# Two more products of q, k and v by quarters, shared PSUM banks, a later softmax quotient and another order in the last group

## The chip, the cores and the metric

The kernel runs on one core of a Trainium2 chip. Its time is the device time of one execution in microseconds (us); lower is better. The engines of the core are TensorE (PE in the profile, its weight loads PEld), VectorE (DVE), ScalarE (ACT), GpSimd (POOL) and SyncE (SP), which issues the DMAs. Each has its own queue of instructions and runs it in order; they meet by semaphores.

## The reference

There are 64 graphs of 256 nodes with 512 features, and one adjacency matrix for all. Layer 0 is a graph convolution, layer 1 an attention with 8 heads of 64 features, where the adjacency matrix makes an additive mask. Everything is fp32.

```
h = relu(layernorm(x))
x = x + (adj @ h) @ W0 + b0
h = relu(layernorm(x))
q, k, v = h @ Wq + bq, h @ Wk + bk, h @ Wv + bv
scores = q k^T / 8 + (1 - adj) * -1e9            # per head
x = x + softmax(scores) v @ Wo + bo
```

## The kernel before

**Groups.** Two graphs make a group (512 tokens), so there are 32 groups. Layer 0 runs over all of them first, then layer 1. In layer 1 the loop at L1132 repeats this order on PE, written out by hand: `attend(g, 0)`, `score(g, 1)`, q and k of group g + 1, `attend(g, 1)`, `score(g + 1, 0)`, v of g + 1, and the output projection o of g. The order in which the program names instructions is the order in each engine's queue (`manual_schedule`).

**Ticks.** Each of q, k, v, o is a Python generator with seven steps; after every step `tick()` advances a clock by one. `after(delay, fn)` puts a piece of work on a list, and the tick at which it is due names its instructions: behind that step's own instructions and ahead of the next step's, on whichever engines it uses. So a delay moves work in the queues of DVE, ACT and POOL against the steps of PE.

**Seven products.** A projection multiplies a 512 x 512 weight by 512 features of 512 tokens. Both are cut into halves, and seven half-size products (Strassen's scheme in Winograd's form) take the place of eight. With the weight's parts a11, a12, a22, s1 to s4 and the tokens' parts b11, b21, b22, t1 to t4 (block sums and differences), the products are P1 = a11 b11, P2 = a12 b21, P3 = s4 b22, P4 = a22 t4, P5 = s1 t1, P6 = s2 t2, P7 = s3 t3. `product` (L453) makes one of them by four matmuls of 256 columns. In groups 2 to 31 (`FIRST2`, L508) `project2` cuts P2, P3 and P4 once more by the same scheme: seven quarter-size products, each one matmul of 128 columns (L564), take the place of four matmuls of 256. This asks for more sums of weights (`block_sums`, once), of tokens (`Blocks.sums`, POOL, each group), and for more additions of results (`add`, L665, DVE; `first`, L907 and L924, ACT).

**Banks.** PSUM, where PE puts its results, has eight banks. `bank()` takes the one that has been free for longest, `give()` returns it. A bank asked for with `seed` has first a copy of SBUF data written to it by ACT (L255), and PE adds to that. `project2` holds at most six banks, one for each of its three inner products' common sums among them; `attend` holds two (`po`) for the unscaled result of the attention until `divide` has read them.

**The softmax.** `score` makes the scores (PE, L974), scales and masks them (DVE, L980, eight instructions), subtracts a bound (POOL, L986, four instructions of 128 x 1024), takes the exponential (ACT, L991, due at the ticks `exps`) and adds up pairs of keys (POOL, L998, due at `sum_delay` and the three ticks behind it). `attend` makes the denominators (PE, L1007) and the product with v (PE, L1014); ACT copies the denominators (L1023), DVE inverts them in four pieces (L1027), two at once and two in `divide`, where also the quotient is formed (L1045). `divide` is due one tick behind `attend`, that is behind the scores. `note` (ACT, L1039) sums up the reciprocals for a check of range.

**Buffers.** Input, residual and hidden tiles of 128 x 2048 come from a pool of four (`xpool`).

Of the kernel before, what the change touches and what calls it, by code (L numbers as in the profile page):

```python
# [13 lines left out]
P = 128  # L14
# [184 lines left out]
def kernel(  # L199
# [33 lines left out]
    main = ExitStack()  # L233
    const = main.enter_context(tc.tile_pool(name="const", bufs=1))
    dram = main.enter_context(tc.tile_pool(name="between", bufs=1, space=bass.MemoryType.DRAM))
    xpool = main.enter_context(tc.tile_pool(name="x", bufs=4))
    act = main.enter_context(tc.tile_pool(name="act", bufs=1))
    tmp = main.enter_context(tc.tile_pool(name="tmp", bufs=3))
    small = main.enter_context(tc.tile_pool(name="small", bufs=4))
# [8 lines left out]
    def bank(shape, name, seed=None):  # L248

        i = next(i for i in free_banks if seed is None or whole[i])  # L250
        free_banks.remove(i)
        t = psum.tile(shape, F32, tag=f"bank{i}", name=name)
        bank_of[id(t)] = (i, t)
        if seed is not None:
            nc.scalar.copy(t, seed[:, None, :].to_broadcast(shape))  # L255
        return t

    def give(t, all_written=True):
# [30 lines left out]
        return xt[32 * i:32 * i + 32, k * NT:(k + 1) * NT, :]  # L289

    def load(g):
        X[g] = xpool.tile([P, T, D], F32, tag="x", name=f"x_{g}")
        for k in range(GB):
            for i in range(NI):
                nc.sync.dma_start(blocks_of(X[g], i, k), by_block(x[g * GB + k], i))
# [212 lines left out]
    FIRST2 = 2  # L508
    W2, spare = {}, []

    def block_sums(n):

        todo = []
        for a in ONCE:
            w = W[n][a]
            def part(i, j):
                return w[:, j, i * P:(i + 1) * P]
            s1, s2, s4 = (spare.pop(0) for _ in range(3))
            W2[n, a] = dict(a11=part(0, 0), a12=part(0, 1), a22=part(1, 1), s1=s1, s2=s2, s3=part(1, 0), s4=s4)
            for o, p, q, op in ((s1, part(1, 0), part(1, 1), ALU.add), (s2, s1, part(0, 0), ALU.subtract),  # L520
                                (part(1, 0), part(0, 0), part(1, 0), ALU.subtract), (s4, part(0, 1), s2, ALU.subtract)):
                todo.append((nc.gpsimd.tensor_tensor, o, p, q, op))
        return todo

    class Blocks:

# [11 lines left out]
            eng.tensor_tensor(t[..., 2, :], self.operand("b22"), t[..., 0, :], op=op)  # L538
            eng.tensor_tensor(t[..., 3, :], self.operand("b21"), t[..., 2, :], op=op)

    def project2(n, halves, blocks, by_token, name, place, first, done=None, seeds=(), add_up=False):

        s = W[n]

        def part(t, i, k):

            m, h = (k, i) if by_token else (i, k)
            t = t if m is None else t[:, m:m + 1, :]  # L550
            return t.rearrange("p m (h j) -> p (m h) j", j=P) if h is None else t[:, :, h * P:(h + 1) * P]

        class Inner:

# [102 lines left out]
        for p, c in zip(inner, ((0, 0), (1, 0), (0, 1))):  # L657
            p.u3()
            p.add(p.sum, None, 1)
            give(p.shared, False)  # L660
            complete(*c)
        yield

    def add(o, ps, u):
# [187 lines left out]


    H1T, HH, HO = {}, {}, {}

    def load_hidden(g):
        H1T[g] = xpool.tile([P, GB, DC, N], F32, tag="x", name=f"h1T_{g}")
        for k in range(GB):
            nc.sync.dma_start(H1T[g][:, k].rearrange("p d n -> p (d n)").rearrange("p (i n) -> p i n", n=N // NI),
                              HT[g][:, :, :, k, :].rearrange("p d i n -> p (d i) n"))  # L860

    def load_residual(g):
        X[g] = xpool.tile([P, T, D], F32, tag="x", name=f"x1_{g}")
        nc.sync.dma_start(X[g], X1[g].rearrange("k (t p) d -> p (k t) d", p=P))

    def hidden_sums(g, *steps):
# [4 lines left out]

    H2, O2 = {}, {}

    def block_hidden(g, step):

        t = act.tile([P, GB, 4, P], F32, tag="t2", name=f"t2_{g}")
        t4 = act.tile([P, 4, P], F32, tag="t24", name=f"t24_{g}")
        x = H1T[g][:, :, 2:4, :].rearrange("p k c (n j) -> p k c n j", j=P)
        H2[g] = block_sums_of(x, t, HH[g], t4, nc.gpsimd, step)

    def block_outputs(g, eng, step):
        x = OT[g][:, 2:4, :].rearrange("p c (k n j) -> p k c n j", k=GB, j=P)
# [8 lines left out]
    def block_sums_of(x, t, halves, t4, eng, step):  # L891
# [3 lines left out]
        after(step + 1, last.sums, eng)  # L895
        return {"b21": Blocks(x[:, 0], t[:, 0]), "b22": Blocks(x[:, 1], t[:, 1]), "t4": last}

    def queries_keys(g):

        for n, store in (("q", Q), ("k", K)):  # L900
            store[g] = {}
            bias = L1[n][1]

            def first(o, ps, i, m=None):
                for c in range(2) if m is None else (m,):
                    to, src = (o[:, c, :], ps[:, c, :]) if m is None else (o, ps)
                    nc.scalar.activation(to, src, AF.Identity, bias=bias[:, 2 * i + c:2 * i + c + 1])  # L907

            def place(i, k):
                if (i, k) not in store[g]:  # L910
                    store[g][i, k] = act.tile([P, 2, N], F32, tag=f"{n}{i}{k}", name=f"{n}_{g}_{i}{k}")
                return store[g][i, k]

            if g < FIRST2:
                yield from project(W[n], HH[g], False, f"{n}_{g}", place, first)
            else:
                yield from project2(n, HH[g], H2[g], False, f"{n}_{g}", place, first)

    def values(g):
        v = act.tile([P, HQ, GB, NT, HF], F32, tag="yT0", name=f"v_{g}")  # L920
        V[g] = {(i, k): v[:, i, k] for i in range(HQ) for k in range(GB)}

        def first(o, ps, i, m=None):
            nc.scalar.copy(o, ps)  # L924

        def place(i, k):
            return V[g][i, k]

        if g < FIRST2:
            yield from project(W["v"], HH.pop(g), True, f"v_{g}", place, first)  # L930
        else:
            yield from project2("v", HH.pop(g), H2.pop(g), True, f"v_{g}", place, first)

    def quarter_of(batch, i):
        return batch.rearrange("(t p) d -> p t d", p=P)[:, :, i * HF:(i + 1) * HF]
# [64 lines left out]
    def attend(g, qd):  # L1000
# [25 lines left out]
        def invert(c):  # L1026
            nc.vector.reciprocal(rden[:, c * P:(c + 1) * P], den[:, c * P:(c + 1) * P])  # L1027

        early = 2 if g >= FIRST2 and (g, qd) != (NG - 1, 1) else 4
        for c in range(early):  # L1030
            invert(c)
        if qd == 0:

            last = g == NG - 1
            OT[g] = (xpool if last else act).tile([P, DC, GN], F32, tag="x" if last else "r", name=f"oT_{g}")
            HO[g] = Halves(f"o_{g}", [OT[g][:, :, k * N:(k + 1) * N] for k in range(GB)], 0 if last else 1)

        def note():
# [2 lines left out]
        def divide():  # L1041
            for c in range(early, 4):
                invert(c)
            for f in range(2):
                nc.vector.tensor_tensor(OT[g][:, 2 * qd + f, :], po[f], rden, op=ALU.mult)  # L1045
                give(po[f])
            after(2 if (g, qd) == (NG - 1, 1) else 3, note)
            wait = 0
            if qd == 0:
                HO[g].sums(nc.gpsimd, ("t1",))  # L1050
            elif g < NG - 2:
                HO[g].sums(nc.gpsimd, ("t3", "t2", "t4"))
            elif g == NG - 2:
                wait = 8
                after(7, HO[g].sums, nc.gpsimd, ("t3",))
                after(8, HO[g].sums, nc.vector, ("t2",))
                after(8, HO[g].sums, nc.gpsimd, ("t4",))
            else:
                HO[g].sums(nc.vector, ("t3", "t2"))
                HO[g].sums(nc.gpsimd, ("t4",))  # L1060
            if qd and g >= FIRST2:
                block_outputs(g, nc.gpsimd, wait + 1 if g >= NG - 2 else 2)

        after(1, divide)

    def run(gen, steps=99):

# [68 lines left out]
    for g in range(NG):  # L1136
        attend(g, 0)
        load_residual(g)
        if g + 2 < NG:
            load_hidden(g + 2)  # L1140
        score(g, 1, *((5,) if g < NG - 1 else (3, (3, 4, 5, 6))))
        tick()
        if g == 0:
            for n, tag in ((4 * DC, "w0_sb"), (4, "w0_s1"), (4, "w0_s2"), (4, "w0_s4"), (4, "adjT"), (4, "b0_r")):
                t = const.tile([P, n, P], F32, tag=tag, name=f"spare_{tag}")
                spare.extend(t[:, i, :] for i in range(n))
        for n, at in (("q", 7),) if g == 0 else (("k", 1), ("v", 5)) if g == 1 else (("o", 2),) if g == 2 else ():
            for i, work in enumerate(block_sums(n)):
                after(at + i // 3, *work)
        if g + 1 < NG:  # L1150
            run(queries_keys(g + 1))
        else:
            last = post(g - 1, seed_outputs(g - 1))
            run(last, 6)
        attend(g, 1)
        if g + 1 < NG:
            score(g + 1, 0, 5)
            tick()
            steps = values(g + 1)
            run(steps, 5)  # L1160
            seeds = seed_outputs(g) if g + 2 < NG else None
            run(steps)
            if g + 2 < NG:
                hidden_sums(g + 2, 2, 3, 4, 5)
                if g + 2 >= FIRST2:
                    block_hidden(g + 2, 6)
                run(post(g, seeds))
# [48 lines left out]
```

## Time and profile before

| | |
|---|---|
| time, median of 3 runs | 2661.51 us (2660.09 to 2661.95) |
| profiled execution: its own time | 2660.45 us |
| its span, first to last instruction | 2658.7 us |
| granted TensorE clock | 0.999 |
| layer 1, one group (group 13) | 63.0 us |
| of it q, k, v, o | 11.70 us each |
| of it a pair of scores / of attend | 3.65 us / 4.45 us, each twice |
| q, k, v of group 1 (no quarters) | 12.2 us each |
| from v of group 31 to the end | 55.8 us |

In a line of the profile, "128x512 f32<-128x512 f32 x4" is the shape of output and input (partitions x elements) and how many instructions there were; a group of lines in the timeline is merged, so "x2" behind a duration is two instructions in that time. What stands in square brackets is the time for which the engine had been idle before, and who ended that. One fp32 matmul of the program makes two records of PE. PE's ends are modelled, and the time by which one matmul follows another is the surer number.

### The profile page before, as it was taken

How to read it: one execution, taken by the hardware profiler on the slowest of the kernel's cores; microseconds unless marked ns; L12 is line 12 of the kernel's file. 1: busy time of each engine (PE TensorE's matmuls, PEld its weight loads, DVE VectorE, ACT ScalarE, POOL GpSimd, SP SyncE). 2: the span in 40 equal slices, each digit the busy share in tenths (PEclk: the TensorE clock that was granted, in tenths of full speed). 3: DMA queues.
4: the chain of work that ended last, by engine and by line, in shares of the span. 5: the costliest groups of instructions: out<-in, count | busy, mean ns of one | idle time of the engine just before them, and what ended most of it. 6: DMA issues, size and time to landing. Idle time of an engine off the chain costs nothing. (4 is left out here: it accounts for less than half of the span.)

```text
span 2658.7 us, 51781 instructions
## 1 busy us (share of the span) xinstructions
PE 2624.0 (99%) x20076; PEld 2282.2 (86%) x20076; DVE 1869.5 (70%) x3864; ACT 970.5 (37%) x1875; POOL 1981.1 (75%) x1838
## 2 busy tenths in 40 slices
PE   7999999999999999999999999999999999999997
PEld 6999899998888888888888888888888888888886
DVE  5878888885467676667677676667677676666677
ACT  3445454443333333333333333333333333333332
POOL 5888888775788777777777777777777777777775
PEclk9999999999999999999999999999999999999999
DMA  5777666665122111111111111111222111111110
GB/s 132 199 193 187 172 166 175 175 158 127 34 60 51 49 49 48 49 49 49 49 48 49 49 49 49 49 48 51 62 66 62 50 49 48 49 49 49 49 48 34
DMA packets 281066, 211.04 MB, mean 79 GB/s; under 512 B 145904, under 2 KB 212976, under 8 KB 280816
## 3 DMA queue, kind: packets, MB, share of 16 engines
q1 hardware_dynamic: 280352, 207.15, 29.9%
q8 instruction: 161, 2.64, 0.4%
q14 instruction: 89, 0.73, 0.1%
q10 hardware_dynamic: 464, 0.52, 0.1%
HBM read 106.96 MB, written 100.66 MB: 78 GB/s over the span
## 5 line engine op out<-in xcount | busy, mean ns | idle before, releaser
L986 POOL TENSOR_TENSOR a<-a,top 128x1024 f32<-128x1024 f32 x253 | 591.2, 2369 | 478.0 <-DVE a L980 478.0
L980 DVE SCALAR_TENSOR_TENSOR a<-sc,maskT 128x512 f32<-128x512 f32 x512 | 311.8, 680 | 122.8 <-PE sc L974 122.8
L998 POOL TENSOR_TENSOR as<-a 128x512 f32<-128x512 f32 x256 | 318.5, 1276 | 3.0 <-ACT a L991 3.0
L991 ACT ACTIVATE a<-a 128x1024 f32<-128x1024 f32 x256 | 270.9, 1058 | 4.3 <-DVE a L984 2.3
L1027 DVE RECIPROCAL rest<-rest 128x128 f32<-128x128 f32 x256 | 224.3, 919 | 36.1 <-ACT rest L1023 36.1
L974 PE MATMUL sc<-q,k 64*128 64x256 f32 x2048 | 239.0, 383 | 0.0
L1014 PE MATMUL pav<-a,v 128*32 128x256 f32 x4096 | 233.6, 379 | 0.0
L974 PEld LDWEIGHTS sc<-q,k 64*128 64x128 f32 x2048 | 194.7, 187 | 44.9 <-issue 26.3
L1014 PEld LDWEIGHTS pav<-a,v 128*32 128x32 f32 x4096 | 133.4, 110 | 87.9
L1023 ACT ACTIVATE rest<-pden 128x512 f32<-128x512 f32 x64 | 38.2, 597 | 417.7 <-PE pden L1007 417.7
L665 DVE TENSOR_TENSOR k<-k,k 128x128 f32<-128x128 f32 (+1 forms) x300 | 96.0, 352 | 126.3 <-PE k L564 123.9
L42 DVE BATCH_NORM_STATS2 st<-x 128x6 f32<-128x512 f32 x256 | 173.1, 676 | 9.4 <-DMA x<-in_x_dram 7.2
L693 ACT ACTIVATE h<-x,nb,rs 128x512 f32<-128x512 f32 x128 | 93.9, 803 | 69.3 <-POOL nb L54 69.2
L820 ACT ACTIVATE h<-x,nb,rs 128x512 f32<-128x512 f32 x128 | 97.2, 808 | 52.2 <-POOL nb L54 49.0
L665 DVE TENSOR_TENSOR x<-o,x 128x128 f32<-128x128 f32 (+1 forms) x360 | 110.9, 349 | 3.4 <-PE o_24b L564 0.3
L665 DVE TENSOR_TENSOR q<-q,q 128x128 f32<-128x128 f32 (+1 forms) x300 | 96.0, 352 | 14.0 <-PE q L564 11.7
L665 DVE TENSOR_TENSOR v<-v,v 128x128 f32<-128x128 f32 (+1 forms) x300 | 95.3, 351 | 14.4 <-PE v L564 11.3
L754 POOL TENSOR_TENSOR hs<-h 128x512 f32<-128x512 f32 x31 | 39.4, 1270 | 73.8 <-ACT h L693 63.7
L446 POOL TENSOR_TENSOR t_o<-oT,t_o 128x512 f32<-128x512 f32 x62 | 79.2, 1277 | 12.3 <-DVE t_o L446 10.0
L446 POOL TENSOR_TENSOR t_y<-yT 128x512 f32<-128x512 f32 (+1 forms) x65 | 81.8, 1258 | 5.9 <-ACT yT L804 5.9
L446 POOL TENSOR_TENSOR t_h<-h1T,t_h 128x512 f32<-128x512 f32 x64 | 82.0, 1282 | 5.0
L52 POOL TENSOR_TENSOR rs<-rs,mhalf 128x2 f32<-128x2 f32 (+1 forms) x97 | 79.5, 820 | 8.1
(4808 smaller groups left out, 6981.8 us busy)
## 6 DMA issues: line engine op xcount, KB each, us to landing
x<-in_x_dram SPq DMA_DIRECT2D x256, 128.0 KB, 3.1
residual<-x SPq DMA_DIRECT2D x256, 128.0 KB, 2.5
hidden<-r SPq DMA_DIRECT2D x128, 256.0 KB, 4.4
h1T<-hidden SPq DMA_DIRECT2D x64, 512.0 KB, 9.7
x<-residual SPq DMA_DIRECT2D x32, 1024.0 KB, 7.7
out_dram<-x SPq DMA_DIRECT2D x62, 512.0 KB, 4.3
w_sb<-in_L_gnn_weight_dram SPq DMA_DIRECT2D x1, 1024.0 KB, 9.8
wq_sb<-in_L_gnn_Wq_dram SPq DMA_DIRECT2D x1, 1024.0 KB, 8.2
```

What stands on the lines that cost most here:

```text
L42: nc.vector.bn_stats(st, src)
L446: eng.tensor_tensor(self.t[n][:, c, :], self.operand(p, c), self.operand(q, c), op=ALU.subtract)
L665: nc.vector.tensor_tensor(o, ps, u, op=ALU.add)
L693: nc.scalar.activation(H0[g][:, t, :], xt[:, t, :], AF.Relu, bias=nb[:, t % n:t % n + 1], scale=rs[:, t % n:t % n + 1])
L820: nc.scalar.activation(h1[:, k * NT + t, :], xt[:, k * NT + t, :], AF.Relu, bias=nb[:, t:t + 1], scale=rs[:, t:t + 1])
L974: nc.tensor.matmul(ps[j][:, kt * N:(kt + 1) * N], k[j * HD:(j + 1) * HD, c, kt * P:(kt + 1) * P], q[j * HD:(j + 1) * HD, c, :], start=(kt ...
L980: nc.vector.scalar_tensor_tensor(a[:, j * NT:(j + 1) * NT, :].rearrange("p k n -> p (k n)"), ps[j], SCALE, maskT_f, op0=ALU.mult, op1=ALU.add)
L986: nc.gpsimd.tensor_tensor(a, a, top_b, op=ALU.subtract)
L991: nc.scalar.activation(a, a, AF.Exp)
L998: nc.gpsimd.tensor_tensor(AS[c, b], a4[:, :, 0, :], a4[:, :, 1, :], op=ALU.add)
L1014: nc.tensor.matmul(po[f][h * 32:(h + 1) * 32, b * N:(b + 1) * N], v[:, k, h * HD + f * 32:h * HD + f * 32 + 32], A[h // 2, b][:, (h % 2) * ...
L1027: nc.vector.reciprocal(rden[:, c * P:(c + 1) * P], den[:, c * P:(c + 1) * P])
```

## The change

`project3` takes the place of `project2` for q, k and v of groups 2 to 31: P1 and P7 are made by quarters too, so five of seven products are, and only P5 and P6 stay half-size. The results of P1 and P7 are built in the outputs c00 and c11; the sums which P6 and P5 are added to are seeded by ACT from there. The running sums of P1, P7 and P3 (A1, A7, A3) share one bank, those of P2 and P4 (A2, A4) another. o keeps `project2`.

For this, two more block sums of tokens are made per group on POOL: `block_first` of b11, due twelve ticks behind the scores of qd 1, and in `block_hidden` those of t3, due two ticks ahead of those of b21 and b22. More weight sums are made (20 instructions in each of q, k and v instead of 12), those of k on DVE. Their room comes from the fourth x buffer, so that layer 1 turns three buffers (`next_x`). The bias of k and q is turned once into a difference.

`divide` is due four ticks behind `attend` where the next group uses `project3`, that is behind step three, all of it but the two early reciprocals. The exponentials are due at 5, 6, 6, 7 and the key sums from 7 on. In the last group the quotient of qd 0 is due a tick later, that of qd 1 at once; the sums of group 30's attention results are due at one tick, ahead of the last group's scores; five steps of o of group 30 stand ahead of the last `attend` where there were six.

```diff
-    xpool = main.enter_context(tc.tile_pool(name="x", bufs=4))
+    xpool = main.enter_context(tc.tile_pool(name="x", bufs=1))
...
+    BUILT = {"a11": "b11", "s3": "t3", **ONCE}
+    SECOND = {"q": BUILT, "k": BUILT, "v": BUILT, "o": ONCE}
...
+    def project3(n, halves, blocks, by_token, name, place, first):
...
+        def take(o, src, i, k, h):
+            first(part(o, i, k), src, h, i)
+
+        def own_added(o, t):
+
+            more(o, part(t, None, 0), None, 0)
+            more(o, part(t, 1, 1), 1, 0)
+
+        def own_taken(o, t, h):
+            first(part(o, None, 1), part(t, None, 1), h, None)
+            give(t)
+
+        c00, c01, c10, c11 = (place(i, k) for i in range(2) for k in range(2))
+        sa = bank([P, 4, P], f"{name}s")
+        a1, a7, a3 = (sa[:, i:i + 1, :] for i in range(3))
+        mm(a1, "a11", "a11", "b11", True)
+        mm(a7, "s3", "a11", "b11")
+        o1 = bank([P, 2, N], f"{name}o1")
+        own(o1, "a11")
+        o7 = bank([P, 2, N], f"{name}o7")
+        own(o7, "s3")
+        take(c00, a1, 0, 0, 0)
+        take(c11, a7, 0, 0, 1)
+        yield
+        mm(a1, "a11", "s2", "t2")
+        mm(part(o1, 1, 1), "a11", "s3", "t3")
+        mm(a7, "s3", "s2", "t2")
+        mm(part(o7, 1, 1), "s3", "s3", "t3")
+        mm(a3, "s4", "a11", "b11")
+        o3 = bank([P, 2, N], f"{name}o3")
+        own(o3, "s4")
+        take(c00, a1, 1, 0, 0)
+        take(c11, a7, 1, 0, 1)
+        take(c01, a3, 0, 0, None)
+        for o, t, h in ((c00, o1, 0), (c11, o7, 1)):
+            own_added(o, t)
+            own_taken(o, t, h)
+        yield
+        mm(a1, "a11", "s1", "t1")
+        mm(a7, "s3", "s1", "t1")
+        mm(a3, "s4", "s2", "t2")
+        mm(part(o3, 1, 1), "s4", "s3", "t3")
+        more(c00, a1, None, 1)
+        take(c01, a3, 1, 0, None)
+        pa = bank([P, 2, N], f"{name}a", seed=c00)
+        more(c11, a7, None, 1)
+        yield
+        o2 = bank([P, 2, N], f"{name}o2")
+        own(o2, "a12")
+        s24 = bank([P, 4, P], f"{name}s24")
+        a2, a4, c4 = (s24[:, i:i + 1, :] for i in range(3))
+        mm(a4, "a22", "a11", "b11", True)
+        mm(a2, "a12", "a11", "b11")
+        mm(a3, "s4", "s1", "t1")
+        take(c10, a4, 0, 0, None)
+        pc = bank([P, 2, N], f"{name}c", seed=c11)
+        more(c00, a2, 0, 0)
+        own_added(c01, o3)
+        yield
+        product(pa, s, "s2", halves, "t2", by_token, start=False, stop=False)
+        first(part(c10, 1, 0), part(pa, 1, 0), None, 1)
+        first(part(c10, None, 1), part(pa, None, 1), None, None)
+        more(c10, part(pa, 0, 0), 0, 0)
+        own_taken(c01, o3, None)
+        more(c01, a3, None, 1)
+        give(sa, False)
+        yield
+        own(pc, "a22", False)
+        mm(a2, "a12", "s2", "t2")
+        mm(part(o2, 1, 1), "a12", "s3", "t3")
+        mm(a4, "a22", "s2", "t2")
+        mm(c4, "a22", "s3", "t3")
+        more(c00, a2, 1, 0)
+        more(c10, a4, 1, 0)
+        more(c10, c4, 1, None)
+        more(c00, part(o2, 1, 1), 1, 0)
+        add(c00, o2, c00)
+        give(o2)
+        add(c10, pc, c10)
+        give(pc)
+        yield
+        product(pa, s, "s1", halves, "t1", by_token, start=False)
+        mm(a2, "a12", "s1", "t1")
+        mm(a4, "a22", "s1", "t1")
+        add(c11, pa, c11)
+        add(c01, pa, c01)
+        give(pa)
+        more(c00, a2, None, 1)
+        more(c10, a4, None, 1)
+        give(s24, False)
+        yield
...
+    def next_x():
+
+        turn[0] += 1
+        return f"x{(turn[0] - 1) % 3}"
...
+    def block_first(g, step):
+
+        x = H1T[g][:, 0, 0:2, :].rearrange("p c (n j) -> p c n j", j=P)
+        H2[g] = {"b11": Blocks(x, tmp.tile([P, 4, P], F32, tag="u", name=f"t11_{g}"))}
+        after(step, H2[g]["b11"].sums, nc.gpsimd)
...
+        H2[g]["t3"] = Blocks(HH[g].t["t3"].rearrange("p c (n j) -> p c n j", j=P),
+                             tmp.tile([P, 4, P], F32, tag="u", name=f"t33_{g}"))
+        after(step - 2, H2[g]["t3"].sums, nc.gpsimd)
...
+    def second(g):
+        return FIRST2 <= g < NG
...
+        delay = 4 if second(g + 1) else 2 if (g, qd) == (NG - 1, 0) else 1
...
             elif g == NG - 2:
-                wait = 8
-                after(7, HO[g].sums, nc.gpsimd, ("t3",))
-                after(8, HO[g].sums, nc.vector, ("t2",))
-                after(8, HO[g].sums, nc.gpsimd, ("t4",))
+                wait = 8 - delay
+                after(wait, HO[g].sums, nc.gpsimd, ("t3",))
+                after(wait, HO[g].sums, nc.vector, ("t2",))
+                after(wait, HO[g].sums, nc.gpsimd, ("t4",))
...
-        after(1, divide)
+        if (g, qd) == (NG - 1, 1):
+            divide()
+        else:
+            after(delay, divide)
...
-        score(g, 1, *((5,) if g < NG - 1 else (3, (3, 4, 5, 6))))
+        score(g, 1, *((7, (5, 6, 6, 7)) if second(g + 1) else (5,) if g < NG - 1 else (3, (3, 4, 5, 6))))
         tick()
+        if g + 2 < NG:
+            block_first(g + 2, 12)
...
-            run(last, 6)
+            run(last, 5)
         attend(g, 1)
         if g + 1 < NG:
-            score(g + 1, 0, 5)
+            score(g + 1, 0, *((5,) if not second(g + 1) else (7, (5, 6, 6, 7)) if g + 2 < NG else (5, (5, 6, 6, 7))))
```

In `project3`, `mm` is one quarter matmul, `own` makes three quarters of an inner product in a bank of its own, `more` is an addition on DVE (L665), `take` a copy or biased copy on ACT, and `part(t, i, k)` the quarter (i, k) of a tile (None for both).

## The prediction

> **What bounds the kernel now.** I read the page's busy table first, then PE's waits, then the timeline of one group of layer 1, because the change lies there.
>
> ```profile
> PE 2624.0 (99%) x20076; PEld 2282.2 (86%) x20076; DVE 1869.5 (70%) x3864; ACT 970.5 (37%) x1875; POOL 1981.1 (75%) x1838
> ...
> PE pa L331 <- DVE adj_p L326: 10.0, 1, 10.0
> PE o_30a L453 <- DVE x L665: 4.0, 1, 4.0
> PE pden L1007 <- POOL as L998: 2.9, 3, 1.3
> ```
>
> PE is never idle except at the start and in the last group: no wait on ACT or DVE stands in the 30 groups between. The chain of waits holds nothing but the last addition, so it gives no path; the order of PE's own work is the path. The stage table of group 13 (us, then PE, PEld, DVE, ACT, POOL busy) says the same: the whole group, then q, k, v, o.
>
> ```profile
> 1417.30:1480.30 63.00, 63.00 (x522) 54.29 (x520) 43.71 (x94) 21.29 (x45) 47.00 (x37) 1.00 0.21 51
> 1425.40:1437.10 11.70, 11.70 (x76) 10.79 (x75) 9.38 (x19) 7.18 (x16) 11.70 (x7) 1.00 0.60 117
> 1437.10:1448.80 11.70, 11.70 (x77) 10.82 (x75) 5.59 (x16) 4.69 (x11) 3.75 (x4) 1.00 0.00 0
> 1456.90:1468.60 11.70, 11.70 (x76) 10.80 (x75) 9.46 (x20) 7.22 (x15) 11.62 (x7) 1.00 0.01 1
> ```
>
> Each projection is 11.70 us of unbroken PE work. So fewer PE slots pay fully, and any new PE wait is paid fully. How such waits arise shows at the end of k of group 13:
>
> ```profile
> 1446.54 0.39 PE L564 MATMUL k<-t,wk_s 128*128 128x128 f32 x2
> 1446.97 0.62 ACT L907 ACTIVATE k<-k,bk_c 128x128 f32<-128x128 f32 x2 [3.31 <-PE k L564]
> 1447.44 0.39 PE L564 MATMUL k_13a<-h1T,spare_w_s 128*128 128x128 f32 x2
> 1447.88 0.39 PE L564 MATMUL k_13a<-t,wk_s 128*128 128x128 f32 x2
> 1448.31 0.37 ACT L907 ACTIVATE k<-k_13a,bk_c 128x128 f32<-128x128 f32 x1 [0.71 <-PE k_13a L564]
> 1448.71 0.62 DVE L665 TENSOR_TENSOR k<-k_13a,k 128x128 f32<-128x128 f32 x2 [0.20 <-ACT k L907]
> ```
>
> ACT at 1448.31 reads the quarter that the matmul of 1447.44 wrote, yet starts only 0.04 us after the last of three matmuls into that bank. DVE at 1448.71 reads other columns of the bank and still starts 0.03 us after ACT's read. At 1446.97 ACT reads the sum, but waits for the later s3 t3 into its shared bank. Order is kept per bank, reads against reads too.
>
> **What the Trainium skill says.** PSUM — Partial Sum Buffer, section "PSUM bank collisions raise a hardware error", tells authors to guard PSUM by bank, not by address, ScalarE reads against VectorE reads included; the lines above agree. The same page, "Engine vs sequencer instructions": ScalarE, VectorE and GpSimd queues are strict FIFO and matmuls start in program order; in the trace too nothing overtakes a waiting instruction. TensorE: Matmul & The Clock Gate, "Wait — 56ns, not 53.3ns?": a warm 128-column matmul takes 55.6 ns of which 2.5 is fixed. Here a quarter matmul's slot is 0.2225 us (four times that), a half product of four 256-column matmuls 1.725.
>
> **The change, part by part.** (1) *PE slots.* A half product by quarters is 7 x 0.2225 = 1.56 instead of 1.725: 0.167 less. Groups 0 and 1, which use no quarters, have 12.18 us per projection against 11.70 with three, so 0.163 each; I take that. Two more in q, k and v: 0.98 us per group, 29.4 us in 30 groups.
>
> (2) *The bank of A1, A7, A3.* I number the projection's matmuls from its start: 35 quarter slots and two half products, 35 x 0.2225 + 2 x 1.725 = 11.24 without a stall. Steps 1 and 2 have eight slots each; A3's first product is slot 12, at 12 x 0.2225 = 2.67, and to be seen at 2.67 + 0.39 + 0.04 = 3.10. The three ACT reads of A1, A7, A3 are issued behind it and so wait for it. In q and k two biased reads and a copy: the pair of 1446.97 took 0.62 with 0.36 for the last, so 0.26 each, and 0.26 for the copy, end 3.89; in v copies 0.17 apart (a pair takes 0.43), end 3.70. Step 3 begins with A1 in this bank, due at 3.56. A restart costs 0.15:
>
> ```profile
> 2624.70 0.73 POOL L539 TENSOR_TENSOR rest<-oT,rest 128x256 f32<-128x256 f32 x1
> 2625.48 0.49 PE L564 MATMUL o_30b<-wo_sb,rest 128*128 128x128 f32 x2 [0.21 <-POOL rest L539]
> ```
>
> Release at 2625.43, weights 0.05 later, and the first record 0.10 longer than 0.275. Stalls: 4.04 - 3.56 = 0.48 in q and k, 0.29 in v: **1.25 a group**. The 0.67 us of A3's other matmuls behind slot 12 is all the cover there is.
>
> (3) *Step 4.* In step 3 DVE adds A1 (0.42), ACT copies A3 (0.26), DVE adds A7 (0.42), by turns on one bank. A3 of step 3 is to be seen at 4.91 (q); then 5.36, 5.70, 6.16, so PE may write A3 at 6.31 against 6.04 due: 0.27 in q and k, 0.22 in v by the same count: **0.76**. Zero if ACT and DVE may read together.
>
> (4) *The quotient.* Behind step 3, DVE's queue gets two reciprocals and two products, with step 4's additions behind them:
>
> ```profile
> 1427.86 1.75 DVE L1027 RECIPROCAL rest<-rest 128x128 f32<-128x128 f32 x2
> 1429.64 1.29 DVE L1045 TENSOR_TENSOR oT<-pav,rest 128x512 f32<-128x512 f32 x2
> 1429.97 1.06 ACT L991 ACTIVATE a<-a 128x1024 f32<-128x1024 f32 x1
> ```
>
> From 6.07 on: 7.82, 9.14, then A2's first addition (0.28, 0.08 of it overlapped) until 9.34. PE's step 6 adds to A2 at 6.53 (step 4's end) + 1.725 + 0.67 = 8.92; released it starts at 9.49: 0.57 in q, the same in v, nothing in k (no quotient there): **1.14**.
>
> (5) *ACT in a bunch.* Exponentials now come behind steps 4, 5, 5, 6, three of them behind the copy of o3, which waits for DVE (10.0 in q). 10.4 plus three of about 1.0 plus the quotient's note (0.61 to the next start) is 13.8. k starts at 11.24 + 1.32 = 12.56, and its second A1 is due at 14.34; but ACT's two first reads of k end at 14.42, and PE restarts at 14.57: 0.23. In v the two seeds of o stand behind two of the exponentials: 12.57 against v's end at 12.32: 0.40. **0.63**, with 0 to 2 as bounds.
>
> (6) *The rest.* DVE gains per projection 2 additions of 128, 3 of 256 and 2 of 512, less one of 384 (0.28, 0.42, 0.69, 0.56): 2.6 us, 43.7 to about 51.5 of a longer group; cover enough but for (4). POOL gains two block sums of 0.73 + 0.46 + 0.46 = 1.65: the first falls into an idle stretch of 15 us in k; the second moves the end of POOL's backlog from q's start to about 1 us into q, whose first use is at 3.3. Cover gone, that is 1 us a group. Key sums stay ahead of the denominators by about 2 us. The three x buffers make the hidden load wait for the previous group's stores (4.3 us, then 9.7 to land) on SP's queue; first use is some 27 us after: nothing. Residual loads stand ahead of it in that queue. Weight sums: 24 more of about 0.46, once, off PE: nothing, up to 5 us. The bias subtraction: nothing. Banks: six and the two of the quotient, eight in all, no spare.
>
> (7) *Last group.* From 2602.9 to the end PE is busy 40.6 of 55.8 us. The DVE sum t2 moves ahead of the scores, the quotient behind step 1's addition (the 4.0 us wait), and g 30's block sums into idle POOL time, so the key sums end about 5 us earlier; one step more of o_30 covers the last quotient. DVE still does 3.0 of quotient and 2.1 of subtraction ahead of step 3's addition, a wait of some 2.7. I take -6, bounds -10 to 0.
>
> **Sum.** 1.25 + 0.76 + 1.14 + 0.63 - 0.98 = 2.80 us per group, 84 in 30. Against the profiled execution, 2660.45 us (span 2658.7): 2660.45 + 84 - 6 = 2738. The median 2661.51 is 1.06 above it, less than the spread of the runs.
>
> **Rivals.** *A, faster:* the reads hide in cover. PE has no wait in 30 groups before, and ACT is busy 37%, which speaks for it; the per-bank order above speaks against. It decides at one place: if the three reads are over by 3.41 (3.56 - 0.15), step 3 has no stall and all behind it moves forward. Then 2660.45 - 29.4 - 6 = 2625. *B, only (2) and a smaller (4):* ACT and DVE read side by side, so (3) goes, the quotient starts earlier (0.37 in q and v) and (5) fits: 1.25 + 0.74 - 0.98 = 1.0, 2685. The 0.20 us wait of DVE on ACT speaks against. *C, ACT becomes the bound at every border:* late exponentials make late key sums, and the denominators wait as in the last group (1.3 us at most there, twice a group): some 50 us more, 2788.
>
> **Numbers.** Forecast 0.48 (its own range 2705 to 2765), A 0.17, B 0.22, C 0.10, no change 0.03 (0.2%, about 5 us, is what a measurement of this kernel can tell from none). Range 2645 to 2770: it leaves out most of A and of C. Faster 0.17, same 0.03, slower 0.80.
>
> **What would show it.** PE waits on ACT before step 3 in q, k, v (0.3 to 0.5), on DVE before step 4's A3 and, in q and v alone, before step 6's A2 (0.6); a projection of 12.4 to 12.7 us. No such waits and 11.37 us means A; waits in step 3 alone mean B. The per-bank reading is what would make it wrong: if ACT starts before slot 12 is done, most of the sum falls.

## The result: slower by 3.3%

The changed kernel takes 2748.98 us (median of 4 runs, 2747.48 to 2749.42) beside 2661.73 us of the kernel before on the same chip (2660.09 to 2662.95): a ratio of 1.0327, interval 1.0309 to 1.0345. The profiled execution has a span of 2747.4 us at a granted clock of 0.997. The forecast was 2738.

First the page's busy table and PE's list of waits, of the changed kernel (total us, number of waits, longest):

```profile
PE 2675.0 (97%) x21156; PEld 2313.4 (84%) x21156; DVE 2091.8 (76%) x4426; ACT 1089.6 (40%) x2445; POOL 2082.5 (76%) x2022
...
PE pa L331 <- DVE adj_p L326: 9.6, 1, 9.6
PE q_2s L682 <- ACT q L1052: 2.6, 2, 2.0
...
PE pden L1156 <- POOL as L1147: 2.3, 3, 1.0
...
PE o_30a L453 <- DVE x L786: 2.1, 1, 2.1
...
PE v_4s L682 <- DVE v L786: 0.3, 1, 0.3
PE v_28s L682 <- DVE v L786: 0.3, 1, 0.3
PE q_5s L682 <- DVE q L786: 0.3, 1, 0.3
```

PE's share falls from 99 to 97%, and its busy time has even grown by 51 us, though its work shrank: with modelled ends part of a wait counts as busy (the last experiment below, with the same matmuls and hardly a wait, has 2596.4). The wait list looks harmless: its tile names hold the group's number, so one wait of 0.3 us that comes back in every group is spread over dozens of small rows. The stage table of one group shows it at once. These are group 13 whole, then its q, k, v, and the output o of group 12 (us, then PE, PEld, DVE, ACT, POOL busy, clock, DMA share, GB/s):

```profile
1453.08:1518.87 65.79, 64.58 (x558) 55.30 (x557) 50.65 (x113) 25.26 (x64) 50.24 (x43) 1.00 0.19 49
1461.19:1473.89 12.70, 12.17 (x89) 11.18 (x88) 10.68 (x26) 8.13 (x20) 12.54 (x9) 1.00 0.51 100
1473.89:1486.19 12.30, 12.07 (x89) 11.05 (x87) 8.32 (x23) 6.06 (x19) 5.63 (x7) 1.00 0.00 1
1494.30:1507.08 12.78, 12.33 (x89) 11.15 (x87) 10.95 (x26) 7.64 (x19) 11.81 (x7) 1.00 0.00 1
1507.08:1518.87 11.79, 11.79 (x75) 10.84 (x75) 8.57 (x22) 2.05 (x4) 11.48 (x13) 1.00 0.01 1
```

The group was 63.00 us and is 65.79, with 2.79 more: 1.00 in q, 0.61 in k, 1.08 in v, 0.10 in o. Attention and scores have not moved. The timeline of q of group 13 at the border of steps 2 and 3 shows the first of the new waits:

```profile
1463.97 0.39 PE L682 MATMUL q_13s<-h1T,wq_s 128*128 128x128 f32 x2
...
1464.39 0.63 ACT L1052 ACTIVATE q<-q_13s,bq_c 128x128 f32<-128x128 f32 x2 [1.83 <-PE q_13s L682]
...
1464.64 0.39 PE L682 MATMUL q_13o<-t,wq_s 128*128 128x128 f32 x2
...
1464.91 0.26 ACT L1049 COPY q<-q_13s 128x128 f32<-128x128 f32 x1
1465.22 0.30 PEld L682 LDWEIGHTS q_13s<-t,spare_w_sb 128*128 128x128 f32 x2 [0.39 <-ACT q L1049]
1465.23 0.38 PE L682 MATMUL q_13s<-t,spare_w_sb 128*128 128x128 f32 x1 [0.20 <-ACT q L1049]
```

The matmul of 1463.97 is A3's. ACT had been idle for 1.83 us, and the last matmul into A1, which it reads first, began at 1463.08; yet it starts at 1464.39, when A3's matmul is over. It doesn't wait for all that the program names ahead of it: o3's three matmuls stand ahead of the read too, and the last of them begins only at 1464.64. Its third read ends at 1465.17, and only then step 3 may write A1. The matmul of 1464.64 has two records 0.11 apart, so the next was due at 1464.86; it comes 0.36 later and its first record is 0.10 too long: 0.47 us lost.

The second new wait comes in step 4 of the same q, where A3 is written again:

```profile
1466.27 0.42 DVE L786 TENSOR_TENSOR q<-q_13s,q 128x256 f32<-128x256 f32 x1
1466.75 0.27 ACT L1049 COPY q<-q_13s 128x128 f32<-128x128 f32 x1
1467.05 0.42 DVE L786 TENSOR_TENSOR q<-q_13s,q 128x256 f32<-128x256 f32 x1 [0.35 <-ACT q L1049]
1467.53 0.49 PE L682 MATMUL q_13s<-t,spare_w_sb 128*128 128x128 f32 x2
```

These are DVE's read of A1, ACT's of A3, DVE's of A7 and the matmul into A3. A3's own reader ends at 1467.02, ahead of the 1467.34 at which the matmul was due. But DVE waits for that reader before it reads A7, until 1467.47, and PE starts 0.06 later; with its first record 0.10 too long, 0.29 us are lost.

The same q at step 6, where A2 is written again:

```profile
1469.18 1.29 DVE L1195 TENSOR_TENSOR oT<-pav,rest 128x512 f32<-128x512 f32 x2
...
1470.38 0.28 DVE L786 TENSOR_TENSOR q<-q_13s,q 128x128 f32<-128x128 f32 x1
1470.58 0.41 DVE L786 TENSOR_TENSOR q<-q_13o,q 128x256 f32<-128x256 f32 x1
1470.72 0.49 PE L682 MATMUL q_13s<-t,spare_w_sb 128*128 128x128 f32 x2 [0.31 <-DVE q L786]
```

DVE's first read of A2 (1470.38) stands behind the quotient and ends at 1470.66; 0.06 later PE starts. The three matmuls before began at 1469.58, so it was due at 1470.25; with a first record again 0.10 too long, 0.57 us are lost.

### The profile page after: what moved, and what is told of

It is laid out like the page before. It is cut to its first block, busy times and chain, and to the rows that moved or that the text cites. A ratio compares the mean times of both kernels' runs of the same rounds, so it can differ in the third digit from the quotient of the medians.

```text
span 2747.4 us, 54804 instructions
## 1 busy us (share of the span) xinstructions
PE 2675.0 (97%) x21156; PEld 2313.4 (84%) x21156; DVE 2091.8 (76%) x4426; ACT 1089.6 (40%) x2445; POOL 2082.5 (76%) x2022
## 5 line engine op out<-in xcount | busy, mean ns | idle before, releaser
L1140 ACT ACTIVATE a<-a 128x1024 f32<-128x1024 f32 x256 | 260.7, 1055 | 3.3 <-POOL a L1135 3.2
L446 POOL TENSOR_TENSOR t_o<-oT 128x512 f32<-128x512 f32 x63 | 81.0, 1286 | 29.5 <-DVE oT L1195 29.5
L947 DVE STREAM_TRANSPOSE r<-h 128x512 f32<-128x512 f32 x128 | 82.8, 684 | 2.1 <-ACT h L941 1.7
L1195 DVE TENSOR_TENSOR oT<-pav,rest 128x512 f32<-128x512 f32 x128 | 82.3, 685 | 2.1
```

Of the source, the lines that this page charges most:

```text
L446: eng.tensor_tensor(self.t[n][:, c, :], self.operand(p, c), self.operand(q, c), op=ALU.subtract)
L1140: nc.scalar.activation(a, a, AF.Exp)
```

## Experiments

The kernel before, timed again beside each of these runs, has medians between 2659 and 2661 us; ratios are given against them. "Group" is the mean period of groups 3 to 30 in the profile, from q to q: 63.02 us before, 65.81 after.

**A3 three slots later: is order kept by bank or by address?**

```diff
-        mm(a3, "s4", "a11", "b11")
         o3 = bank([P, 2, N], f"{name}o3")
         own(o3, "s4")
+        mm(a3, "s4", "a11", "b11")
```

> The changed kernel with step 2's A3 matmul behind the three of o3 instead of ahead of them: one line moved by three slots of 0.22 us, nothing else. Theory (order by bank): ACT may not read A1 and A7 before A3's matmul has written the bank, 0.67 us later than now, so step 3 waits 0.67 us longer in each of q, k and v: 2.0 us in each of 29 groups, about 2808 us, between 2795 and 2820. Rival (order by address): the reads of A1 and A7 start at once as they would with A3 in another bank, and step 3's wait stays or falls: 2749 or less.

2806.26 us (2804.62 to 2809.12), 1.0551, interval 1.0533 to 1.0568; group 67.82, or 2.01 more. The timeline of q of group 13 in this kernel:

```profile
1486.21 0.39 PE L682 MATMUL q_13s<-h1T,wq_s 128*128 128x128 f32 x2
1486.64 0.63 ACT L1052 ACTIVATE q<-q_13s,bq_c 128x128 f32<-128x128 f32 x2 [2.50 <-PE q_13s L682]
...
1487.15 0.27 ACT L1049 COPY q<-q_13s 128x128 f32<-128x128 f32 x1
...
1487.47 0.38 PE L682 MATMUL q_13s<-t,spare_w_sb 128*128 128x128 f32 x1 [0.87 <-ACT q L1049]
```

ACT's idle time grew by just the 0.67 us by which A3 was moved, and so did PE's wait. A read of A1 waits for a matmul that has nothing to do with A1 but the bank. Order by address is refuted. One PSUM tile of the program fills a bank here, so an order by tile would look the same. (The wait is one on a semaphore, and the program decides what it waits for; whether the chip itself would have needed it, this run doesn't tell.)

**A3 one step later in the same bank.** Its three matmuls go from steps 2, 3, 4 to 3, 5, 6, and two quarters of step 6 to step 4; A7's matmul of step 2 goes a slot earlier. Steps 2 to 4 in short:

```diff
-        mm(a3, "s4", "a11", "b11")
...
-        take(c01, a3, 0, 0, None)
...
-        mm(a3, "s4", "s2", "t2")
+        mm(a3, "s4", "a11", "b11")
...
-        take(c01, a3, 1, 0, None)
...
         more(c11, a7, None, 1)
+        take(c01, a3, 0, 0, None)
...
-        mm(a3, "s4", "s1", "t1")
+        mm(part(o2, 1, 1), "a12", "s3", "t3")
+        mm(c4, "a22", "s3", "t3")
...
-        own_added(c01, o3)
```

Step 5 gets A3's second matmul behind `product` and `own_added(c01, o3)`, step 6 its third.

> The changed kernel with A3's three matmuls one step later each, in the same bank, and the fourth quarters of A2 and A4 two steps earlier; the same matmuls, adds and copies. Theory (reads and matmuls of one bank are kept in order, so A3 between the reads of A1 and A7 makes step 3 and step 4 wait): the waits at step 3 (0.47, 0.47, 0.29 us) and step 4 (0.29, 0.29, 0.27) go, step 6's gets shorter by about 0.3 in q and v, while the late starts of k and o grow by about 1 us together because ACT has the two copies of o3 later; about 1.5 us less in each group, 2705 us, between 2690 and 2725. Rival (order by address, the waits come of DVE and ACT being late in general): no gain from moving A3, 2745 or more.

2695.77 us (2693.75 to 2698.77), 1.0139, interval 1.0122 to 1.0156; group 63.96, or 1.85 less. In q, k and v of group 13 the waits at steps 3 and 4 are gone; what is left is 0.34 at step 6 of q (0.57 in the changed kernel), 0.60 in k's first reads and 0.99 at the start of o. So the two bank waits go, and what ACT has to do late grows, as expected; the gain is 0.35 a group larger than expected.

**All reciprocals at the attention, so that the quotient is short.**

```diff
-        early = 2 if g >= FIRST2 and (g, qd) != (NG - 1, 1) else 4
+        early = 4
```

> The changed kernel with all four reciprocals of a quotient issued right behind the attention, so that behind step 3 only the two products of 0.65 us stand (about 1.3 us of DVE instead of about 3). Theory (the long quotient behind step three holds back the DVE reads of step 4, hence step 6's A2, and bunches the ACT reads ahead of k and o): the step-6 wait of about 0.57 us in q and v and the late starts of k (0.18) and o (0.39) go, 1.7 us in each of some 29 groups; about 2698 us, between 2685 and 2712. Rival (the stalls are only the bank order of A1, A7 and A3, and the quotient's length is idle filler): 2749 within 5 us. Rival (the reciprocals delay the reads of the scores, which stand behind them on DVE): 2755 or more.

2697.26 us (2696.80 to 2698.97), 1.0143, interval 1.0126 to 1.0159; group 64.09, or 1.72 less. The waits of steps 3 and 4 stand unchanged (0.47 and 0.28 in q). The timeline of q of group 13 at the quotient and step 6:

```profile
1447.31 1.28 DVE L1195 TENSOR_TENSOR oT<-pav,rest 128x512 f32<-128x512 f32 x2
...
1448.50 0.28 DVE L786 TENSOR_TENSOR q<-q_13s,q 128x128 f32<-128x128 f32 x1
...
1450.16 0.39 PE L682 MATMUL q_13s<-t,spare_w_sb 128*128 128x128 f32 x2
```

DVE reads A2 1.4 us ahead of PE's need, and step 6 has no wait. q is 0.58 shorter, k 0.19, v 0.85, o 0.10: the terms of the step-6 wait and of the late starts. The reciprocals cost nothing at their new place, where DVE waits for the scores.

**The quotient back behind the attention.**

```diff
-        delay = 4 if second(g + 1) else 2 if (g, qd) == (NG - 1, 0) else 1
+        delay = 1 if second(g + 1) else 2 if (g, qd) == (NG - 1, 0) else 1
```

> The changed kernel with the quotient one step behind the attention again (two reciprocals and two products ahead of step 2's reads) instead of behind step 3. Theory (DVE's reads of o1 and o7 in step 2 come 3 us late, and with them the reads of A1 and A7 that step 3 and step 4 wait for; in exchange the waits at step 6 and at the starts of k and o go): 2.7 us more in q and in v, about 2.4 us more in each of 29 groups on balance, 2819 us, between 2795 and 2840. Rival (the quotient behind step three is what makes the kernel slower): 2735 or less.

2803.61 us (2802.97 to 2805.13), 1.0535, interval 1.0517 to 1.0552; group 67.62, or 1.81 more where 2.4 was expected. In q of group 13 step 4 now waits 2.05 us for DVE in place of 0.29; step 6 and the starts of k and o wait no more. q grows by 1.18, v by 0.92. The 2.7 that was expected for q and v is too much: it is near the whole of the stalls (2.5 in q) and not their growth. With the quotient at its full length, the later place is the better of the two in this kernel.

**Both edits together**, and ACT's copy of o3 moved one step ahead of DVE's additions.

> Both edits, and the ACT copy of o3's right column moved one step ahead of its DVE adds. Theory: no wait is left inside q, k and v in a steady group, so that only the saving of 0.98 us in each group stands against the kernel before; 2749 less 3.8 times 29, about 2640 us, between 2630 and 2660, faster than the kernel before by 0.5 to 1.1%. Rival (DVE and ACT, which carry the adds and copies of two more quarter-size products, bound the projections themselves): the waits come back at other places, 2690 or more.

2648.16 us (2647.13 to 2650.16), 0.9957, interval 0.9940 to 0.9973: faster than the kernel before. The group is 62.40. In group 13 this leaves 0.31 in k (its first two reads stand behind the note on ACT's queue) and 0.09 in o of group 12 (PE waits for a sum of POOL). DVE and ACT have the same work as in the changed kernel, so their load was not the bound (DVE 50.1 us and ACT 25.3 in a group, against 50.7 and 25.3).

**The work ahead of group 2.** Its q took 17.2 us, 4.5 more than the later ones. The timeline of the changed kernel there, from two narrow windows; a merged row's end is its start and its us together:

```profile
733.39 4.79 POOL L1135 TENSOR_TENSOR a<-a,top 128x1024 f32<-128x1024 f32 x2
734.50 1.26 DVE L1065 TENSOR_TENSOR bq_c<-bq_c 128x2 f32<-128x2 f32 x1
735.69 2.63 DVE L276 TENSOR_TENSOR wk_sb<-wk_sb 128x128 f32<-128x128 f32 x2
735.80 0.37 ACT L1052 ACTIVATE q<-q_2s,bq_c 128x128 f32<-128x128 f32 x1 [2.55 <-DVE bq_c L1065]
...
735.89 4.79 DVE L276 TENSOR_TENSOR wk_sb<-wk_sb 128x128 f32<-128x128 f32 x2
738.14 2.40 POOL L1135 TENSOR_TENSOR a<-a,top 128x1024 f32<-128x1024 f32 x1
```

The subtraction of two columns takes 1.26 us and holds ACT, whose second read of q needs the new bias. Then two sums of k's weights end at 738.32 and 740.68, each some 0.15 us behind the end of a POOL instruction (738.18 and 740.54). Their ends follow POOL's and not their own size (0.28 us alone), so DVE doesn't slow down there; it stands still until POOL is done (the last section has this for more sizes). The Trainium skill says so: SBUF — State Buffer, section "Who interferes with whom", has a VectorE instruction with two SBUF inputs and a GpSimd one that reads SBUF exclude each other for the whole of an instruction. Behind these sums stand DVE's reads of q.

```diff
-                if g == FIRST2:
-
-                    nc.vector.tensor_tensor(bias[:, 2:4], bias[:, 2:4], bias[:, 0:2], op=ALU.subtract)
...
+            for n in "qk":
+                row = L1[n][1]
+                after(20, nc.vector.tensor_tensor, row[:, 2:4], row[:, 2:4], row[:, 0:2], ALU.subtract)
...
-        for n, i, at in ((("q", 0, 4), ("q", 1, 9), ("k", 0, 9)) if g == 0 else
-                         (("k", 1, 1), ("v", 0, 3), ("v", 1, 8)) if g == 1 else
+        for n, i, at in ((("q", 0, 4), ("q", 1, 9), ("k", 0, 9), ("k", 1, 20)) if g == 0 else
+                         (("v", 0, 3), ("v", 1, 8)) if g == 1 else
```

> The changed kernel with the two bias subtractions and the in-place sums of k's weights done by DVE while group 1's values run, instead of at the head of group 2. Theory (group 2's late start is these DVE instructions, two to five times longer beside POOL's mask subtraction, ahead of the reads of q's and k's first products): q of group 2 falls from 17.2 to about 12.8 us and k from 13.3 to 12.3, the kernel by 4 to 6 us to about 2744; the sums take what they may at their new place, where project needs DVE less. Rival (group 2 starts late because its own block sums or the weights' sums on POOL come late): q of group 2 stays above 16 us.

2742.90 us (2741.71 to 2746.45), 6.1 less than the changed kernel's 2748.98; 1.0312, interval 1.0295 to 1.0329. In the profile, from q of group 2 to q of group 3 it is 64.6 us and no longer 70.8; q of group 2 takes 12.1, k 12.1. At the new place DVE waits for POOL no less, as its instructions there tell (ns min/median/max):

```profile
L276 DVE TENSOR_TENSOR wk_sb<-wk_sb x4: 280/1055/1359, 707.8 to 711.2; 128x128 f32<-128x128 f32 x4
L276 DVE TENSOR_TENSOR bq_c<-bq_c x1: 1125/1125/1125, 706.7 to 706.7; 128x2 f32<-128x2 f32 x1
```

but POOL's instructions there are sums of 1.3 us and not subtractions of 2.4. The place isn't free either. DVE's additions for the output of group 0 stand behind these sums, and PE's list of waits has a new row:

```profile
PE o_0a L453 <- DVE x L786: 1.1, 1, 1.1
```

This output takes 13.5 us in place of 12.2, so of the 6.2 us won in group 2 some 4.9 remain; the 6.1 between the medians can't be told from that.

**The last group's order as it was.**

```diff
-        delay = 4 if second(g + 1) else 2 if (g, qd) == (NG - 1, 0) else 1
+        delay = 4 if second(g + 1) else 1
...
-            after(3, note)
+            after(2 if (g, qd) == (NG - 1, 1) else 3, note)
...
-        if (g, qd) == (NG - 1, 1):
-            divide()
-        else:
-            after(delay, divide)
+        after(delay, divide)
...
-            run(last, 5)
+            run(last, 6)
```

> The changed kernel with the last group's order as it was: six steps of group 30's output ahead of the last attention, its quotient one step later, the note as before. Theory (the other order saves less than the 6 us forecast, because the time that it takes out of group 30's output, 4.8 us, comes back in the last attention and in the last output): from the start of the last group's first attention to the end 49.1 us in place of 47.5, the kernel 1 to 2 us longer, 2750 or 2751, which the times alone can't tell from 2749. Rival (the forecast's 6 us): 53 us and 2755.

2747.10 us (2746.07 to 2747.49), 1.0322, interval 1.0305 to 1.0339, and in the profile from the last group's first attention to the last matmul (the tail) 45.0 us in place of 47.5. Both the theory (49.1) and its rival (53) had it longer. The other order costs 2.4 us in the profiles (the medians are 1.9 apart): with it the last attention comes earlier and PE waits there 1.1 us for key sums, a wait that the old order doesn't have. What the tail gained on the kernel before came from something else. One thing left of the change there is that group 30's sums t2, t4 and its block sums are due a step earlier, ahead of the last scores. That alone, in the kernel before:

```diff
-                after(8, HO[g].sums, nc.vector, ("t2",))
-                after(8, HO[g].sums, nc.gpsimd, ("t4",))
+                after(7, HO[g].sums, nc.vector, ("t2",))
+                after(7, HO[g].sums, nc.gpsimd, ("t4",))
...
-                block_outputs(g, nc.gpsimd, wait + 1 if g >= NG - 2 else 2)
+                block_outputs(g, nc.gpsimd, 7 if g == NG - 2 else wait + 1 if g == NG - 1 else 2)
```

> The kernel before with group 30's last sums of the attention output and their block sums one step earlier, as the change has them: ahead of the last group's second scores instead of behind them. Theory (this earlier start is what the tail gains, 4.1 us by the difference of the kernel before, 49.1, and e_last_order, 45.0): from the last group's first attention to the end 45 us, group 30's output from 16.1 to about 14 us, the kernel about 4 us shorter, 2656. Rival (the tail gains by the shape of the new projections or by the score's later exponents): the tail stays at 48 us or more.

2654.03 us (2653.45 to 2657.27), 0.9977, interval 0.9968 to 0.9986 (3.7 to 8.5 us less): in the profile the tail is 44.5 in place of 49.1, group 30's output 13.95 in place of 16.12. In its list of waits the 4.0 us of before have become

```profile
PE o_30a L453 <- DVE x L665: 2.2, 1, 2.2
```

**A kernel that beats both.** e_best has both edits of the projection, the earlier work for group 2, the first note of a group two steps later, and the last group's DVE subtraction of its first scores on POOL; the second run puts the last group's order back as well.

> e_a3_moved_recips and three more moves: the note of the first quotient of a group two steps later (out of the way of k's first two reads), the work before group 2 as in e_group2, and the last group's third mask subtraction on POOL as in the other groups. Theory: k's last wait (0.29 us in each of 29 groups, 8.4 us) goes, with about 4.5 us of group 2 and 1.4 us of the last group's values: 2648 less 14, about 2634 us, between 2628 and 2644; steady group 62.1 us. Rival (the note falls on another wait of k, and the sums collide with other work in group 1): 2645 or more.

2632.66 us (2631.50 to 2633.56), 0.9892, interval 0.9876 to 0.9909.

> e_best with the last group's order as it was before the change (as in e_last_order). Theory (the other order costs 2.4 us and what the tail won came of the sums that start one step earlier): from the last group's first attention to the end 44.7 us in place of 47.1, so 2630 us, between 2627 and 2634. Rival (with the shorter projections the sums come late again ahead of the old order's sixth step): the tail at 47 us or more, 2633 or more.

2629.93 us (2629.70 to 2630.39), 0.9888, interval 0.9871 to 0.9904; the tail is 44.6, and 47.1 in e_best, so the old order wins 2.4 us here too. The stage table of this kernel, group 13 and then its q, k, v and o of group 12:

```profile
1408.06:1470.16 62.10, 62.10 (x558) 54.47 (x557) 50.15 (x113) 25.23 (x64) 50.22 (x43) 1.00 0.20 52
1416.16:1427.54 11.38, 11.38 (x89) 10.96 (x88) 8.73 (x23) 8.00 (x20) 11.22 (x9) 1.00 0.54 106
1427.54:1438.90 11.36, 11.36 (x89) 10.82 (x87) 8.10 (x22) 6.34 (x19) 7.48 (x8) 1.00 0.01 1
1447.01:1458.38 11.37, 11.37 (x89) 10.96 (x87) 8.74 (x23) 7.66 (x19) 11.29 (x7) 1.00 0.00 0
1458.38:1470.16 11.78, 11.78 (x77) 10.66 (x75) 9.06 (x23) 1.84 (x4) 11.46 (x13) 1.00 0.01 1
```

PE's busy time is the stage's length again, and ACT and DVE do the same work as in the changed kernel. Each of q, k and v is 0.33 below the 11.70 of before: the whole of the slots saved, and no stall. Of the 30 us won against the kernel before, 4.5 are won in the tail, about as much as the earlier sums win alone, and these don't need the quarters. The 1.3 us in the output of group 0 (13.5) are still lost here.

## Why the forecast held, and what it mis-sized

The forecast was right, by the mechanism it named: 2749 lies in its range of 2705 to 2765, and the waits stand where it put them. Measured in group 13 by the spacing of the matmuls, against its terms:

| term | forecast, us a group | measured |
|---|---|---|
| (1) slots saved | -0.98 | -0.99 (e_best_order: 11.70 less 11.37, three times) |
| (2) step 3, bank of A1, A7, A3 | 1.25 | 1.22 (0.47, 0.47, 0.29) |
| (3) step 4, A3 | 0.76 | 0.85 (0.29, 0.29, 0.27) |
| (4) step 6, A2 behind the quotient | 1.14 | 1.14 (0.57 in q and v, none in k) |
| (5) ACT in a bunch | 0.63 | 0.56 (0.18 in k, 0.38 in o) |
| sum | 2.80 | 2.79 |

That A3 causes (2) and (3) is shown by moving it both ways. That the bank is the reason is shown for (2) by e_a3_last; for (3) it is read from the timeline above, where the last reader before PE's start is A7's and ACT and DVE read by turns, as the forecast's walk had it. (4) and (5) are shown to be the quotient by shortening it. The 0.09 too little in (3) is the largest error of the five, and that the sum agrees to 0.01 us is luck: (2) and (5) err the other way. q, k and v take 12.70, 12.30 and 12.78 us, a little wider than the 12.4 to 12.7 foreseen.

Rival A (2625) and rival B (2685) fall with the waits themselves: B wanted no wait at step 4. Rival C (late denominators) falls too: PE's waits on key sums are 2.3 us in all, less than the 2.9 of before.

The span grew by 88.7 us. The 28 periods between group 3's q and group 31's hold 78.2 of it. Two terms at the ends of layer 1 were mis-sized, both too low, and make up 9.9 of the 10.6 us between the forecast (2738.4) and the profiled execution (2749.0):

- (6), "Weight sums: 24 more of about 0.46, once, off PE: nothing, up to 5 us. The bias subtraction: nothing." From group 2's q to group 3's the time grew by 7.35 and not by 2.80: 4.6 us more, by DVE instructions behind POOL's. The step took their durations from rows in which they ran alone, and didn't ask what stands behind them on DVE. e_group2 shows that they cost even more, 6.2: without them this period is only 1.1 longer than before, not 2.80, because the quotient of group 1 has all four reciprocals early in every one of these kernels, so that group 2 doesn't have the stalls of (4) and (5).
- (7), "I take -6, bounds -10 to 0". From the end of the last v to the end of the span it is 0.7 less (55.0 and 55.7 us), and 1.7 to the last matmul. The earlier sums alone are worth 4.7 to the last matmul in the kernel before (e_before_sums), but the other order that the term counted as a gain costs 2.4 (e_last_order), and the last group's first attention takes 0.5 longer. Behind the last matmul stand stores and closing instructions, 6.6 us before and 7.5 now; they vary between 6.6 and 7.6 in the twelve profiles, and no run ties this to the change.

The last group's v is 0.9 longer than the others, besides. In e_best, which moves the subtraction of its scores from DVE to POOL, it is 11.5, close to the other v's 11.37; that edit was not run alone, so the cause is likely and not shown.

## What to carry to other kernels

Before small accumulators are put into one bank, write down the order of every matmul and every read of that bank: a reader waits for a matmul into its neighbour, and the next matmul waits for that reader (moving A3 by a step and other matmuls and reads around it, with no work added, was worth 1.85 us in every group). Of work that is moved behind a step, count its length against the time until PE needs the first thing queued behind it: the same quotient without two reciprocals was free. And look for a repeated stall in a stage table, since a list of waits by tile name may cut it into rows too small to notice.

## What the runs showed of the hardware that was not expected

A DVE addition of two SBUF operands of 128x128, 0.28 us alone, took up to 2.44 us beside POOL's 128x1024 subtraction: the time until POOL's instruction ended and 0.15 more. What remains behind POOL's end goes by the size. For 2, 128, 512 and 1024 elements in a partition it was 0.02, 0.15, 0.55 and 1.08 us (the bias and k's weights in the changed kernel; t_o and the subtraction of the last group's scores on DVE in the kernel before), about 1.04 ns an element. Beside the same subtractions DVE's masking of the scores, which has one operand in PSUM, took 0.68 to 0.69 in all of its 512 instructions.

It works the other way too. In the last group of the kernel before, DVE's sum t_o of 128x512 took 1.87 us, since it came 1.3 us ahead of the end of a POOL subtraction; in the changed kernel it comes first and takes 0.73, and POOL's sum that began 0.13 us later takes 1.74 in place of 1.28. The trace of before showed this already. The "2.1 of subtraction" in the forecast is the mean of DVE's three subtractions there (1.73, 2.23 and 2.23), each of which ends 1.08 us behind the end of a POOL instruction; the forecast took it for a plain duration.
